# Four graph layers on one core: a third row buffer for the first two layers, and three small moves around it

## The chip, the core and the metric

The kernel runs on one core of a Trainium2 chip. A core has five engines that run their own instruction queues in order: TensorE (PE; its weight loads are shown as PEld), VectorE (DVE), ScalarE (ACT), GpSimd (POOL) and SyncE (SP), which here only issues DMA transfers. They meet at semaphores. The metric is device time in microseconds, the median of several runs.

## The reference, cut to what matters

Sixteen graphs of 1024 nodes with 128 features go through four layers. Each layer first normalises every node's features and clips at zero, and adds its result to `x`.

```python
h = relu(layernorm(x));  x = x + L0(h, adj, adj)   # rows: sum_i adj[i,j] h[i] / sum(adj[j,:]), two weights, relu
h = relu(layernorm(x));  x = x + L1(h, adj)        # (adj / row sums) @ h @ W1, leaky relu
h = relu(layernorm(x));  x = x + L2(h, adj)        # two rounds of an edge network: sigmoid scores on
                                                   # the edges, messages, a two-layer update, a layernorm
h = relu(layernorm(x));  x = x + L3(h, adj)        # attention: exp over the edges, row sums, elu
```

L2 needs, for each pair of nodes with an edge, `relu(a[i] + b[j]) . w` and its sigmoid. The graph has few edges, so the kernel compresses each 128x128 block of the adjacency to at most 320 slots (480 on the diagonal) by matrices of zeros and ones that TensorE multiplies with.

## The kernel before, in words

One graph is a *batch*. Its work is cut into three pieces, each a generator that emits instructions and yields a weight of progress:

- `first` (L721): layers 0 and 1, the norm ahead of layer 2, and then `build` (L828), which makes the 0/1 matrices `on`, `onT`, `om`, `omT` of 36 blocks (28 off the diagonal, 8 on it), four blocks to a group, nine groups.
- `main` (L1169): layer 2. Each of its two rounds (`round`, L890) walks over the nine groups: `gather` (L991, matmuls `pre` at L1001, ACT and DVE make `hid` at L1017 and L1018), `dots` (L1034), `scores` (L1060, DVE's `val` at L1091), `scatter` (L1096, matmuls `p` at L1113, DVE's `upd` at L1121) and `messages` (L1130). Between the rounds `between` (L1152) updates the nodes by halves.
- `last` (L1199): the end of layer 2 and layer 3.

`run` (L1225) weaves three batches into one another: while `main` works on batch b, `last` ends batch b-1 and `first` starts batch b+1. The weave decides in which order instructions are emitted; the framework then gives out buffers and orders each engine's queue by that emission order, by what is ready and by which buffers it takes to be free. The order is fixed in the program. Buffers with one tag form a ring: `bufs` says how many, and a tile waits until an older one of its tag has had its last reader.

What the change touches:

- **Row buffers** (`N_ROW`, L36; `row`, L694; `load`, L688). A row buffer of 4 KB per partition holds one strip of the adjacency. Layer 0 reads for each of eight tiles t a row strip `at` and a column strip `ct` (loads at L738 and L742, recorded at L691); layer 1 reads a strip `l` of the transposed matrix. All of them come from the tag `rowa` with two buffers. For `at`, ACT sums the rows (L744, output `tn`, sum `deg`), TensorE transposes it (L748), ACT copies the halves out (L749), and the result is stored (L751, `adjT<-tn`). For `ct`, DVE takes the pattern of edges (L756, `has`) and TensorE multiplies it with the features (`neighbours`, L290, `nb`), and DVE adds the product, scaled by the reciprocal `rdeg` of the row sum, to `own` (L315).
- **The reciprocal** of the row sum stands at L745, between ACT's sum and the transposes.
- **Spare hot buffers** (`MORE_OFF`, L39; `hot_tile`, L798). The 0/1 matrices of the 28 blocks off the diagonal have 28 + 4 buffers of each of the four kinds, so that `build` for the next batch can run ahead of `main`, which still reads the old ones. Those on the diagonal have eight and no spare.
- **Norm statistics** (`spread`, L227): per-partition statistics from eight (or four) `bn_stats`, then seven small DVE instructions of 8 (or 4) elements, a power of -0.5 on POOL (L243) in their midst, and one more small instruction in `normal` (L250) before ACT may normalise (L252). `spread` runs eight times per batch: ahead of each of the four layers (`normal`), and in four half updates (`update`, L338).
- **The half update of half 1**. `between` starts by loading the features of its half from DRAM (`back`, L717, shown at L718 as `xm<-xT`). `main` makes the generator at L1195 but takes its first step only in the second round, at the first group.
- **Weights**: `we2_rows` (L106, L111) has its own buffer for the whole kernel though only `fold_weights` uses it.

Of the kernel before, what the change touches and what calls it, by code (L numbers as in the profile page):

```python
# [9 lines left out]
F32 = mybir.dt.float32  # L10
# [4 lines left out]
OP = mybir.AluOpType  # L15
AX = mybir.AxisListType

LN_EPS = 1e-5
# [14 lines left out]

LANES = ("m", "a", "c")
N_SCRATCH = {"m": 5, "a": 4, "c": 5}
N_ROW = {"m": 2, "a": 2, "c": 1}  # L36
N_HID = 6

MORE_OFF = 4  # L39
MORE_DIAG = 0  # L40


# [9 lines left out]
def tile_four_gnn_layers(  # L52
# [22 lines left out]
    nc = tc.nc  # L75
    B, N, D = x.shape
    P = 128
# [3 lines left out]
    L = we1.shape[0]  # L81
# [10 lines left out]
    const = ctx.enter_context(tc.tile_pool(name="const", bufs=1))  # L92
# [10 lines left out]
    nc.scalar.dma_start(b0_bc, b0[None, :].broadcast_to([P, D]))  # L103
    we1_sb = const.tile([P, L, 2, D], F32, name="we1_sb")
    we2_sb = const.tile([P, L], F32, name="we2_sb")
    we2_rows = const.tile([P, L, D], F32, name="we2_rows")  # L106
    be1_sb = const.tile([P, L], F32, name="be1_sb")
    scale_sb = const.tile([P, L, 2], F32, name="scale_sb")
    with nc.allow_non_contiguous_dma(reason="small columns of weights, once"):
        nc.scalar.dma_start(we2_sb, we2.rearrange("l d o -> d (l o)"))  # L110
        nc.scalar.dma_start(we2_rows, we2.rearrange("l d o -> (o l) d")[None].broadcast_to([P, L, D]))  # L111
        nc.scalar.dma_start(be1_sb, be1.rearrange("l d -> d l"))
        nc.scalar.dma_start(scale_sb[:, :, 0], gamma.rearrange("l d -> d l"))
        nc.scalar.dma_start(scale_sb[:, :, 1], beta.rearrange("l d -> d l"))
# [41 lines left out]
            nc.tensor.transpose(wT_ps[:, k], w01_sb[:, k], ident)  # L156
        nc.vector.tensor_copy(wT, wT_ps)

    def fold_weights():


        signs = slide[:, :, G - 1]
        nc.scalar.activation(signs, we2_sb, AF.Sign)
        nc.vector.tensor_mul(we2_sb, we2_sb, signs)
        nc.vector.tensor_mul(be1_sb, be1_sb, we2_sb)
        nc.scalar.activation(we2_rows, we2_rows, AF.Abs)
        for l in range(L):
# [15 lines left out]
    def flat(t):  # L183
        return t.rearrange("p t d -> p (t d)")
# [4 lines left out]
    class Layers:  # L189
# [37 lines left out]
        def spread(self, src, name):  # L227

            n = src.shape[1]
            bn = self.small([P, T, 6], "bn", f"bn_{name}")[:, :n]  # L230
            for t in range(n):
                nc.vector.bn_stats(bn[:, t], src[:, t])

            st = self.small([P, 4, T], "stat", f"st_{name}")[:, :, :n]
            nc.vector.tensor_add(st[:, 0], bn[:, :, 1], bn[:, :, 4])
            nc.vector.tensor_sub(st[:, 1], bn[:, :, 1], bn[:, :, 4])
            nc.vector.tensor_add(st[:, 2], bn[:, :, 2], bn[:, :, 5])
            nc.vector.scalar_tensor_tensor(
                st[:, 1], st[:, 1], D / 4.0, st[:, 1], op0=OP.mult, op1=OP.mult
            )  # L240
            nc.vector.tensor_add(st[:, 1], st[:, 1], st[:, 2])
            nc.vector.tensor_scalar(st[:, 1], st[:, 1], 1.0 / D, LN_EPS, op0=OP.mult, op1=OP.add)
            nc.gpsimd.tensor_tensor(st[:, 2], st[:, 1], half_neg[:, :n], op=OP.pow)  # L243
            nc.vector.tensor_scalar(st[:, 0], st[:, 0], 0.5, None, op0=OP.mult)
            return st[:, 2], st[:, 0], st[:, 3]

        def normal(self, src, dst, func, name):

            rstd, mean, less = self.spread(src, name)
            nc.vector.scalar_tensor_tensor(less, mean, -1.0, rstd, op0=OP.mult, op1=OP.mult)  # L250
            for t in range(T):
                nc.scalar.activation(  # L252
                    dst[:, t], src[:, t], func, scale=rstd[:, t : t + 1], bias=less[:, t : t + 1]
                )
# [83 lines left out]
        def update(self, l, xf, xfT, msgT, dst, name):  # L338

            h2 = flat(self.scratch(f"h2s_{name}")).rearrange("p (k n) -> p k n", k=KB)  # L340
            for kb in range(KB):
                ps = self.one(f"h2_{name}_{kb}")
                for i, src in enumerate((xfT, msgT)):
                    nc.tensor.matmul(  # L344
                        ps, wu1_sb[:, l, i, kb * P : (kb + 1) * P], src,
                        start=(i == 0), stop=(i == 1),
                    )
                nc.scalar.activation(h2[:, kb], ps, AF.Relu, bias=bu1_sb[:, l, kb : kb + 1])
                yield 2
            new = self.scratch(f"xn_{name}")[:, :Q]  # L350
            ps = self.one(f"xn_{name}")
            for kb in range(KB):
                nc.tensor.matmul(
                    ps, wu2_sb[:, l, kb], h2[:, kb], start=(kb == 0), stop=(kb == KB - 1)
                )
            nc.scalar.activation(flat(new), ps, AF.Identity, bias=bu2_sb[:, l : l + 1])
            yield 2
            ps = self.one(f"tx_{name}").rearrange("p (t d) -> p t d", d=P)
            for t in range(Q):
                nc.tensor.transpose(ps[:, t], new[:, t], ident)  # L360
            nc.vector.tensor_add(dst, ps, xf)
            yield 1
            rstd, mean, _ = self.spread(dst, f"y_{name}")
            for t in range(Q):
                nc.vector.tensor_scalar(
                    dst[:, t], dst[:, t], mean[:, t : t + 1], rstd[:, t : t + 1],
                    op0=OP.subtract, op1=OP.mult,
                )
            yield 2
            nc.vector.tensor_mul(dst, dst, over_t(rows["gamma"][:, l], Q))  # L370
            nc.vector.tensor_add(dst, dst, over_t(rows["beta"][:, l], Q))
            yield 1
# [157 lines left out]
    class Edges:  # L530
# [76 lines left out]
        def scaled(self):  # L607

            con = self.con
            fold_weights()  # L610
            self.scale_terms()

            w3T = self.a.scratch("w3T")[:, 0]
            ps = self.a.one("w3T")[:, :P]
            nc.tensor.transpose(ps, w3_sb, ident)
            nc.vector.tensor_copy(w3T, ps)
            ps = self.a.one("v3")[:, :2]
            nc.tensor.matmul(ps, w3T, a3_sb, start=True, stop=True)
            nc.vector.tensor_copy(v3, ps)
            spread_v3(0)  # L620
            self.slide = con.tile([P, L, 2 * G - 1], F16, name="slide16")
            nc.vector.tensor_copy(self.slide, slide)
# [71 lines left out]
        def row(self, lane, name):  # L694
# [2 lines left out]
            self.n_rows += 1  # L697
            return self.work.tile([P, T, P], F32, tag=f"row{v}", name=name, bufs=N_ROW[v])

        def alone(self, lane, others):  # L700

            v = lane.lane
            lane.banks = [self.own[w] for w in others or v]
            lane.homes = [(f"h{w}", N_SCRATCH[w]) for w in others or v]
            self.rows_of[v] = others or v

        def columns(self, mat, t):
            return mat[:, t * P : (t + 1) * P].rearrange("(k p) n -> p k n", p=P)
# [12 lines left out]
        def first(self, b):  # L721
# [15 lines left out]
            for t in range(T):  # L737
# [4 lines left out]
                ct = self.load("a", self.columns(adj[b], t), f"ct_{b}_{t}")  # L742
                turned = lane.scratch(f"tn_{b}_{t}")
                nc.scalar.activation(turned, at, AF.Copy, accum_out=deg[:, 0, t : t + 1])  # L744
                nc.vector.reciprocal(rdeg[:, t : t + 1], deg[:, 0, t : t + 1])  # L745
                for ks, ps in lane.halves(f"tn_{b}_{t}"):
                    for i, k in enumerate(ks):
                        nc.tensor.transpose(ps[:, i], at[:, k], ident)  # L748
# [6 lines left out]
                for i, lo, hi in parts:  # L755
                    nc.vector.tensor_tensor(  # L756
                        has[:, i : i + hi - lo], ct[:, lo:hi], turned[:, lo:hi],
                        op=OP.logical_or, saturate=False,
                    )
                lane.layer0_tile(t, ct, z, own, rdeg, name)  # L760
                yield 2
            lane.layer0_end(xt, own)
# [406 lines left out]
        def main(self, s, b):  # L1169
# [7 lines left out]
            for l in range(L):  # L1177
# [11 lines left out]
                def half(h):  # L1189
                    return self.between(  # L1190
                        l, h, self.msg[h], s.xf[h], s.xT[h], xf[h], copy[h], f"{name}_{h}"
                    )

                yield from self.round(s, l, name, before, lambda: half(0))
                before = half(1)  # L1195
                s.xf, s.xT = xf, copy
            s.msg = self.msg

        def last(self, s, b):  # L1199


            def strip(k, lo, hi):
                n = (hi - lo) * P
                at = flat(self.row("c", f"a3_{b}_{lo}_{k}"))[:, : 2 * n].rearrange("p (k n) -> p k n", k=2)
# [230 lines left out]
```

## Time and profile before

| | before |
|---|---|
| time, median of 3 (range) | 5477.2 us (5474.47 to 5483.25) |
| profiled execution | 5482.0 us, granted TensorE clock 0.981 |
| PE busy | 5008.5 us, 91% |
| DVE busy | 4302.6 us, 78% |
| ACT busy | 3055.7 us, 56% |
| POOL busy | 174.4 us, 3% |
| DMA queue of SP | 545.58 MB, 33.7% of 16 engines' span |
| at, ct and l loads | 128 each of 512 KB; median 4.2, 4.5 and 4.3 us from issue to landing |

From the third batch on one weave takes about 331 us. Of the one that begins at 1148 us, layer 0's tiles take the time to 1243 us, layer 1 the time to 1313 us, and the building of the 0/1 matrices the rest to 1479 us; `main` runs beside all three. "Busy" is the time in which at least one instruction of an engine was under way. The view of waits lists what ended each idle stretch of an engine; the chain follows, from the last instruction back, what each step waited for.

### The profile page before, as it was taken

Reading aid. Unit: us, or ns where it says so; the run is one execution under the profiler, and the core shown is the slowest. Engines: PE = TensorE matmul, PEld = TensorE weight load, DVE = VectorE, ACT = ScalarE, POOL = GpSimd, SP = SyncE. Lnnn points to the kernel's source line nnn. Section 1 sums busy time; section 2 is a strip of 40 time slices with the busy share of each in tenths; the row PEclk is TensorE's granted clock in tenths of the full one; section 3 lists DMA queues with packets and bytes.
Section 4 is the critical chain, followed back from the end, with each engine's and each line's share of the span. In section 5 each row is a group of like instructions: output and inputs, shape, how many; then the busy total and the mean of one; then the engine's idle time right before and its main releaser. Section 6 shows DMA issues by size and latency. Waiting matters only on the chain.

```text
span 5482.0 us, 113604 instructions
## 1 busy us (share of the span) xinstructions
PE 5008.5 (91%) x45109; PEld 3741.4 (68%) x45109; DVE 4302.6 (78%) x10759; ACT 3055.7 (56%) x6790; POOL 174.4 (3%) x137
## 2 busy tenths in 40 slices
PE   5989999999999999999999999999999999999996
PEld 4666767667676766767667676676766666677664
DVE  3776787877879778797877878778797887978876
ACT  4556564655646556465555646556465564655543
POOL 0000000000000000000000000000000000000000
PEclk8999999999999999999999999999999999999998
DMA  6242415243252422424234142432424324243121
GB/s 176 63 138 83 124 57 144 78 128 104 73 145 66 135 90 86 137 70 126 91 107 126 57 144 79 125 106 72 146 65 137 90 87 133 68 128 92 54 63 51
DMA packets 740141, 554.56 MB, mean 101 GB/s; under 512 B 32273, under 2 KB 686353, under 8 KB 739601
## 3 DMA queue, kind: packets, MB, share of 16 engines
q1 hardware_dynamic: 734496, 545.58, 33.7%
q8 instruction: 356, 5.83, 0.4%
q10 hardware_dynamic: 5104, 1.65, 0.1%
q14 instruction: 185, 1.51, 0.1%
HBM read 446.44 MB, written 100.66 MB: 100 GB/s over the span
## 4 chain that ended last, share of the span: by engine, by line
PE 49%; DVE 28%; ACT 9%; DMA 8%; issue 4%; POOL 3%; SPq 0%; POOLq 0%; ACTq 0%; DVEq 0%
PE pre L1001 13%; DVE val L1091 8%; PE p L1113 6%; DMA at<-in_adj_dram 5%; DVE hid L1018 4%; PE msg L1130 4%; PE sc L1034 3%; PE bb L298 3%; PE h L344 3%; PE nb L290 3%; ACT hid L1017 2%; PE hp L507 2%; DVE omT L862 2%; POOL st L243 2%; PE pq L858 2%
## 5 line engine op out<-in xcount | busy, mean ns | idle before, releaser
L1018 DVE SCALAR_TENSOR_TENSOR hid<-pre,hid 128x320 f16<-128x320 f32 (+1 forms) x2048 | 1009.2, 507 | 327.5 <-ACT hid L1017 315.9
L1017 ACT ACTIVATE hid<-pre 128x320 f16<-128x320 f32 (+1 forms) x2048 | 906.4, 454 | 547.4 <-PE pre L1001 514.7
L1001 PEld LDWEIGHTS <-part 128*128 128x128 f16 x8192 | 748.6, 98 | 459.3 <-issue 236.6
L1001 PE MATMUL pre<-on,part 128*128 128x320 fp8e4 (+1 forms) x4096 | 970.1, 311 | 70.6 <-DVE hid L1018 62.3
L1001 PE MATMUL pre<-om,part 128*128 128x320 fp8e4 (+1 forms) x4096 | 987.4, 311 | 0.0
L1091 DVE TENSOR_TENSOR val<-onT,u 128x384 f32<-128x384 fp8e4 (+1 forms) x1152 | 603.4, 582 | 3.1
L1130 PE MATMUL msg<-upd,xf 128*128 128x128 f32 (+3 forms) x3008 | 604.7, 321 | 0.0
L1113 PE MATMUL p<-val,omT 128*128 128x128 f16 x6528 | 532.7, 220 | 43.0 <-DVE val L1091 33.7
L1113 PEld LDWEIGHTS <-omT 128*128 128x128 fp8e4 x6528 | 434.5, 97 | 111.5 <-DVE val L1091 42.0
L870 ACT ACTIVATE om<-pm 128x320 fp8e4<-128x320 f32 (+1 forms) x576 | 269.9, 469 | 351.4 <-PE pm L822 347.8
L1091 DVE TENSOR_TENSOR val<-omT,u 128x384 f32<-128x384 fp8e4 x896 | 443.4, 553 | 0.0
L1130 PEld LDWEIGHTS msg<-upd,xf 128*128 128x128 f32 x3008 | 409.8, 192 | 16.0 <-DVE upd L1121 3.0
L1121 DVE SCALAR_TENSOR_TENSOR upd<-p,adj 128x512 f32<-128x512 f32 x512 | 349.8, 683 | 80.8 <-PE p L1113 78.5
L1113 PE MATMUL p<-val,onT 128*128 128x128 f16 x4480 | 378.4, 220 | 0.5 <-DVE upd L1121 0.4
L507 PE MATMUL hp<-wh,e 128*128 128x129 f32 x2048 | 336.0, 289 | 25.5 <-DVE e L503 25.5
L854 ACT ACTIVATE onT<-pn 128x384 fp8e4<-128x384 f32 (+1 forms) x576 | 295.3, 513 | 114.0 <-PE pn L822 95.8
L1113 PEld LDWEIGHTS <-onT 128*128 128x128 fp8e4 x4480 | 307.8, 97 | 51.7 <-issue 16.5
L1055 ACT ACTIVATE srow<-sc,be_s,down 128x128 f32<-128x128 f32 (+2 forms) x512 | 254.6, 536 | 118.2 <-PE sc L1034 117.6
L507 PEld LDWEIGHTS hp<-wh,e 128*128 128x128 f32 x2048 | 281.3, 196 | 55.4 <-DVE e L503 29.8
L1034 PE MATMUL sc<-hid,slide 128*32 128x320 f16 (+1 forms) x4096 | 275.2, 317 | 27.5 <-DVE hid L1018 24.9
L862 DVE TENSOR_TENSOR omT<-pq,odd_off 128x384 fp8e4<-128x384 f32 x448 | 248.7, 555 | 57.5 <-PE pq L858 54.7
L744 ACT ACTIVATE tn<-at 128x1024 f32<-128x1024 f32 x128 | 135.3, 1057 | 270.5 <-DMA at<-in_adj_dram 238.8
(220 smaller groups left out, 8270.1 us busy)
## 6 DMA issues: line engine op xcount, KB each, us to landing
at<-in_adj_dram SPq DMA_DIRECT2D x128, 512.0 KB, 4.2
ct<-in_adj_dram SPq DMA_DIRECT2D x128, 512.0 KB, 4.5
adjT<-tn SPq DMA_DIRECT2D x128, 512.0 KB, 5.1
l<-adjT SPq DMA_DIRECT2D x128, 512.0 KB, 4.3
adj<-adjT SPq DMA_DIRECT2D x256, 256.0 KB, 3.6
a<-adjT SPq DMA_DIRECT2D x128, 384.0 KB, 3.2
adj<-adjT SPq DMA_DIRECT2D x448, 64.0 KB, 2.1
adj<-adjT SPq DMA_DIRECT2D x192, 128.0 KB, 2.6
```

The costliest lines, as they stand in the source:

```text
L507: nc.tensor.matmul(sums[:, t], e[:, i, t * P : (t + 1) * P], wh[:, k + i, : D + 1], start=False, stop=True, skip_group_check=True,)
L854: nc.scalar.activation(onT, pn[:, : ck * P], AF.Copy, saturate=False)
L862: nc.vector.tensor_tensor(omT.rearrange("p (k m) -> p k m", m=P), pq[:, :ck], self.odd[t == u][:, :, None].to_broadcast([P, ck, P]), op=OP ...
L870: nc.scalar.activation(om, pm[:, :c], AF.Copy, saturate=False)
L1001: nc.tensor.matmul(pre[:, :c], path.parts[node // Q][:, k, node % Q, v], hot[:, :c], start=(hot is on and k == 0), stop=(hot is om and k = ...
L1017: nc.scalar.activation(hid[:, 0, :c], pre[:, :c], AF.Relu)
L1018: nc.vector.scalar_tensor_tensor(hid[:, 1, :c], pre[:, :c], 0.0, hid[:, 0, :c], op0=OP.max, op1=OP.subtract)
L1034: ins = nc.tensor.matmul(self.sc[g * G : (g + 1) * G, : self.c], self.path.slide[:, self.l, G - 1 - r : 2 * G - 1 - r], self.hid[self.done ...
L1091: nc.vector.tensor_tensor(pair[:, i % 2, :ck], right[:, :ck], v.to_broadcast([P, ck, P]), op=OP.mult)
L1113: nc.tensor.matmul(self.ps[d][:, i], left[:, k], halves[:, k, :, h], start=(k, h) == terms[0], stop=(k, h) == terms[-1],)
L1121: nc.vector.scalar_tensor_tensor(upd, self.ps[d], S_SCALE, self.adj[:, d * Q : (d + 1) * Q], op0=OP.add, op1=OP.mult,)
L1130: nc.tensor.matmul(self.msg[h][:, (lo - h * Q) * P : (hi - h * Q) * P], self.xf[mb // Q][:, mb % Q], up, start=False, stop=True, skip_grou ...
```

## The change

- `rowa` gets a third buffer. To make room, `MORE_OFF` goes from 4 to 2 (two buffers fewer of each of the four kinds), `we2_rows` moves into a scratch buffer and is loaded when it is used, and the strip buffer of layer 3 gets a tag of its own of 3 KB in place of a row buffer of 4 KB.
- The row sum's reciprocal moves behind the copies and `has`, next to its first reader.
- `spread` takes four small DVE instructions ahead of POOL's power (six before), and one beside it (one before); the factor one half on the mean moves into `normal`'s instruction, and costs one small instruction in `update`.
- `main` takes the first step of half 1's `between` at the end of the first round, so that the load of its features is issued there.
- When one lane runs alone, it takes row buffers in the order a, a, m, a, m (five in all, as before with a, m, c, a, m).

```diff
-N_ROW = {"m": 2, "a": 2, "c": 1}
+N_ROW = {"m": 2, "a": 3, "c": 1}
-MORE_OFF = 4
+MORE_OFF = 2
...
-    def fold_weights():
+    def fold_weights(we2_rows):
...
+        nc.scalar.dma_start(we2_rows, we2.rearrange("l d o -> (o l) d")[None].broadcast_to([P, L, D]))
         nc.scalar.activation(we2_rows, we2_rows, AF.Abs)
...
+            nc.vector.tensor_sub(st[:, 1], bn[:, :, 1], bn[:, :, 4])
+            nc.vector.scalar_tensor_tensor(
+                st[:, 2], bn[:, :, 2], D * LN_EPS, bn[:, :, 5], op0=OP.add, op1=OP.add
+            )
+            nc.vector.scalar_tensor_tensor(st[:, 1], st[:, 1], 0.25, st[:, 1], op0=OP.mult, op1=OP.mult)
+            nc.vector.scalar_tensor_tensor(
+                st[:, 1], st[:, 2], 1.0 / D, st[:, 1], op0=OP.mult, op1=OP.add
+            )
+            nc.gpsimd.tensor_tensor(st[:, 2], st[:, 1], half_neg[:, :n], op=OP.pow)
             nc.vector.tensor_add(st[:, 0], bn[:, :, 1], bn[:, :, 4])
-            nc.vector.tensor_sub(st[:, 1], bn[:, :, 1], bn[:, :, 4])
-            nc.vector.tensor_add(st[:, 2], bn[:, :, 2], bn[:, :, 5])
-            nc.vector.scalar_tensor_tensor(
-                st[:, 1], st[:, 1], D / 4.0, st[:, 1], op0=OP.mult, op1=OP.mult
-            )
-            nc.vector.tensor_add(st[:, 1], st[:, 1], st[:, 2])
-            nc.vector.tensor_scalar(st[:, 1], st[:, 1], 1.0 / D, LN_EPS, op0=OP.mult, op1=OP.add)
-            nc.gpsimd.tensor_tensor(st[:, 2], st[:, 1], half_neg[:, :n], op=OP.pow)
-            nc.vector.tensor_scalar(st[:, 0], st[:, 0], 0.5, None, op0=OP.mult)
...
-            nc.vector.scalar_tensor_tensor(less, mean, -1.0, rstd, op0=OP.mult, op1=OP.mult)
+            nc.vector.scalar_tensor_tensor(less, mean2, -0.5, rstd, op0=OP.mult, op1=OP.mult)
...
+            nc.vector.tensor_scalar(mean, mean, 0.5, None, op0=OP.mult)
...
+        def strip(self, name):
+            if self.rows_of.get("c"):
+                return flat(self.row("c", name))
+            return self.work.tile([P, 2 * 3 * P], F32, tag="strip", name=name, bufs=1)
...
-            self.rows_of[v] = others or v
+            self.rows_of[v] = "aamam" if others else v
...
-                nc.vector.reciprocal(rdeg[:, t : t + 1], deg[:, 0, t : t + 1])
...
+                nc.vector.reciprocal(rdeg[:, t : t + 1], deg[:, 0, t : t + 1])
                 lane.layer0_tile(t, ct, z, own, rdeg, name)
...
                 before = half(1)
+                yield next(before)
```

More of the change, by code (lines that the diff above doesn't have):

```diff
@@ L105, in tile_four_gnn_layers @@
     we2_sb = const.tile([P, L], F32, name="we2_sb")
-    we2_rows = const.tile([P, L, D], F32, name="we2_rows")
     be1_sb = const.tile([P, L], F32, name="be1_sb")
@@ L110, in tile_four_gnn_layers @@
         nc.scalar.dma_start(we2_sb, we2.rearrange("l d o -> d (l o)"))
-        nc.scalar.dma_start(we2_rows, we2.rearrange("l d o -> (o l) d")[None].broadcast_to([P, L, D]))
         nc.scalar.dma_start(be1_sb, be1.rearrange("l d -> d l"))
@@ L234, in spread @@
             st = self.small([P, 4, T], "stat", f"st_{name}")[:, :, :n]
-            nc.vector.tensor_add(st[:, 0], bn[:, :, 1], bn[:, :, 4])
-            nc.vector.tensor_sub(st[:, 1], bn[:, :, 1], bn[:, :, 4])
-            nc.vector.tensor_add(st[:, 2], bn[:, :, 2], bn[:, :, 5])
-            nc.vector.scalar_tensor_tensor(
-                st[:, 1], st[:, 1], D / 4.0, st[:, 1], op0=OP.mult, op1=OP.mult
-            )
-            nc.vector.tensor_add(st[:, 1], st[:, 1], st[:, 2])
-            nc.vector.tensor_scalar(st[:, 1], st[:, 1], 1.0 / D, LN_EPS, op0=OP.mult, op1=OP.add)
-            nc.gpsimd.tensor_tensor(st[:, 2], st[:, 1], half_neg[:, :n], op=OP.pow)
-            nc.vector.tensor_scalar(st[:, 0], st[:, 0], 0.5, None, op0=OP.mult)
+            nc.vector.tensor_sub(st[:, 1], bn[:, :, 1], bn[:, :, 4])
[7 more added lines that the diff above has]
+            nc.gpsimd.tensor_tensor(st[:, 2], st[:, 1], half_neg[:, :n], op=OP.pow)
+            nc.vector.tensor_add(st[:, 0], bn[:, :, 1], bn[:, :, 4])
             return st[:, 2], st[:, 0], st[:, 3]
         def normal(self, src, dst, func, name):
-            rstd, mean, less = self.spread(src, name)
-            nc.vector.scalar_tensor_tensor(less, mean, -1.0, rstd, op0=OP.mult, op1=OP.mult)
+            rstd, mean2, less = self.spread(src, name)
+            nc.vector.scalar_tensor_tensor(less, mean2, -0.5, rstd, op0=OP.mult, op1=OP.mult)
             for t in range(T):
@@ L609, in scaled @@
             con = self.con
-            fold_weights()
+            fold_weights(self.c.scratch("we2_rows")[:, :L])
             self.scale_terms()
@@ L1203, in strip @@
                 n = (hi - lo) * P
-                at = flat(self.row("c", f"a3_{b}_{lo}_{k}"))[:, : 2 * n].rearrange("p (k n) -> p k n", k=2)
+                at = self.strip(f"a3_{b}_{lo}_{k}")[:, : 2 * n].rearrange("p (k n) -> p k n", k=2)
                 nc.sync.dma_start(
```

## The prediction

> **What bounds the kernel now.** I read the page from its engine table to its chain, then the windows of one weave, then the waits of ACT and SP inside it, then the timeline around one of those waits.
>
> ```profile
> PE 5008.5 (91%) x45109; PEld 3741.4 (68%) x45109; DVE 4302.6 (78%) x10759; ACT 3055.7 (56%) x6790; POOL 174.4 (3%) x137
> ...
> PE 49%; DVE 28%; ACT 9%; DMA 8%; issue 4%; POOL 3%; SPq 0%; POOLq 0%; ACTq 0%; DVEq 0%
> PE pre L1001 13%; DVE val L1091 8%; PE p L1113 6%; DMA at<-in_adj_dram 5%; DVE hid L1018 4%; PE msg L1130 4%; PE sc L1034 3%; PE bb L298 3%; PE h L344 3%; PE nb L290 3%; ACT hid L1017 2%; PE hp L507 2%; DVE omT L862 2%; POOL st L243 2%; PE pq L858 2%
> ```
>
> No engine carries the chain alone: TensorE has half of it. One load, `at`, has 5% of it (about 270 us of 5482), though all DMA together is at a third of its engines. The windows show the three stages of the weave that begins at 1148 us (columns: PE, PEld, DVE, ACT, POOL busy, granted clock, DMA share):
>
> ```profile
> 1148.00:1243.00 95.00, 89.31 (x820) 68.16 (x819) 71.70 (x189) 49.78 (x114) 2.64 (x2) 1.00 0.52 151
> 1243.00:1313.00 70.00, 67.35 (x560) 52.77 (x557) 48.32 (x121) 28.36 (x56) 2.64 (x2) 1.00 0.42 124
> 1313.00:1479.00 166.00, 153.51 (x1445) 110.93 (x1444) 147.55 (x362) 111.98 (x255) 5.45 (x4) 0.98 0.23 69
> ```
>
> In the tile stage DVE has 23 us and ACT 45 us to spare; in the building stage DVE is 89% busy. The chain of waits within the tile stage gives `at` 17.5% of its 95 us, 16.6 us: more than any other line there. The waits of ACT over the whole kernel and of SP's queue say why:
>
> ```profile
> ACT tn L744 <- DMA at<-in_adj_dram: 238.8, 93, 5.7
> ...
> DVE deg L745 <- ACT tn L744: 79.1, 63, 3.3
> ...
> SPq L691 <- PE tn L748: 830.8, 123, 26.9
> ...
> SPq L691 <- PE nb L290: 414.0, 156, 13.0
> ```
>
> ACT stands before 93 of 128 row sums until the strip lands. SP could not issue it: with two buffers, the next `at` waits for the transposes of this one. One instance, from the timeline:
>
> ```profile
> 1204.85 0.60 PE L748 MATMUL tn<-ident,at 128*128 128x128 f32 x4
> ...
> 1205.52 0.34 SPq L691 DMA_DIRECT2D at<-in_adj_dram  x1
> ...
> 1208.36 0.37 SPq L691 DMA_DIRECT2D ct<-in_adj_dram  x1
> ...
> 1209.57 1.06 ACT L744 ACTIVATE tn<-at 128x1024 f32<-128x1024 f32 x1 [2.55 <-DMA at<-in_adj_dram]
> ```
>
> The load goes out 0.07 us after the last transpose and lands 4 us later; ACT idles 2.55 us of them, with the `hid` behind it in its queue.
>
> **What the Trainium skill says.** (1) "Perfetto Trace Analysis", Identifying the Most-Contended Engine: matmul busy time misjudges TensorE, since matmuls are pipelined. The trace agrees: `pre` lasts 311 ns, but eight of them take 1.09 us on the chain, 0.136 us each, so 89 busy of 95 us is not full. (2) The same page, Optimization Strategy: the same bubble again and again can mean too few buffers for the next tile; 93 of 128 strips show it. (3) "DMA: Bandwidth & Descriptors", Anatomy of one DMA: about 2 us fixed plus bytes over 436 GB/s, 3.2 us for 512 KB; the trace's median of 4.2 us is used. (4) "Perfetto Trace Analysis", Optimizing Scalar/DVE Operations: some 60 ns of DVE per small instruction, with a profiled latency of about twice that. The trace has 166 ns for a statistics instruction, with starts 80 ns apart; 80 is used.
>
> **The change part by part.**
>
> *Third row buffer.* In the changed program's SP queue, `at` of tile t+1 stands behind the store of t-1 and waits for the product `nb` of t-1, no longer for the transposes of t. In the instance above that is the moment at which `ct` of the next tile went out in the earlier round (1198.02 us), 7.5 us ahead of 1205.52 and over the 4.2 us that it needs. So the wait of ACT, and with it most of DVE's wait at the reciprocal, goes. What is left sets the gain. TensorE's own pace in the tile stage, from counts of the groups in that window and spacings on the chain: 199 `pre` x 0.135 = 26.9, 128 `nb` x 0.115 = 14.7, 222 `p` x 0.057 = 12.7, 64 transposes x 0.11 = 7.0, `msg` 7.0, `sc` 3.5, the other 51 some 10 (512-wide ones at 0.45, the rest at 0.11 to 0.23): 82 us of 95. Layer 1's stage, counted likewise, needs 66.5 of 70: 95%. If the tile stage comes to that, it takes 82/0.95 = 86 us: 9 us less per weave. Thirteen weaves have a tile stage of 95 to 99 us; two (85 and 77 us) get 5 us; the first runs alone with five buffers before and after. 13 x 9 + 2 x 5 = **127 us**. Loads of `l` and `ct` come earlier too, but PE waited for them only 9.3 and 10.4 us in all: within that figure.
>
> *Reciprocal.* It waited for ACT 79.1 us because ACT waited for `at`; behind `has` it waits for something DVE has just waited for. What was queued behind it was `val` and `hid`. Its gain is inside the 9 us. Cost: nothing, the same 128 instructions of 159 ns.
>
> *Statistics.* 64 spreads in `normal` lose two instructions each and 64 in `update` one: 192 x 0.08 = 15.4 us of DVE. The way from the first of them to POOL was 1.17 us (1318.21 to 1319.38); two links of about 0.2 us fall out. Where nothing else fills TensorE (`PE tp L260 <- ACT xf L252`, 55.9 us in all), that shows in full; elsewhere DVE has room outside of the building stage. Between 0 and 0.08 x 12 + 4 x 0.4 = 2.6 us per batch; I take 0.7: **11 us**.
>
> *Half 1's first step.* `xm<-xT` is on the chain once per weave with 3.69 us, issued at 1301.95 us behind four loads of `adj`; PE waits for it 14.0 us in all. Issued some ten places earlier in SP's queue, it is there in time. Between 14 and 15 x 3.7 = 55 us; other chains lie close, so 1.5 us per weave: **22 us**.
>
> *Two spare buffers fewer.* A block's matrices now wait for the block two places back in the old batch's last round, not four. In the changed order, `onT`, `om` and `omT` stand 6 to 9 places later in their queues, about half a group. Today's waits for such a release are small: `DVE on L813 <- PE pre L1001` 23.9 us, and `ACT onT` for `val` 13.6. Lower bound 0, upper bound two blocks' making at the end of each weave (36 blocks take some 150 us of the building stage, 4 us each), 8 us x 15 = 120. I take 1 us per weave: a loss of **15 us**. The work that hides the rest is the diagonal group, which comes last and has no spare in either version.
>
> *Weights.* `we2_rows` is loaded where it is used: ACT, and then DVE and the scales behind it, wait for a landing of 2 to 4 us once, less 0.49 us of issue at the start: a loss of **2 us**. The strip's tag and the lone lanes' order keep their numbers of buffers: nothing.
>
> Sum: -127 - 11 - 22 + 15 + 2 = -143: 5477 - 143 = **5334, say 5335 us**.
>
> **The rivals.**
> - *The wait changes its name.* ACT comes to `tn` early, but TensorE's backlog of `p` and `msg` or DVE's eight `val` (3.75 us in one piece on the chain) then end last. For it: DVE has 12.5% of the stage's chain in `val`. Against it: DVE is 75% busy there. With 3 us per weave left of the 9: 45 + 11 + 1 for the load: 5420 us.
> - *The building stage pays.* DVE is at 89% there, and a late buffer stops an engine with everything queued behind it. With the small gain above (57 us) and 5.5 us lost in 15 weaves (83): 5503 us, slower. Against it: today's waits for these buffers are under 3 us per weave.
> - *All comes off.* The tile stage falls to TensorE's 82 us (13 us x 13 + 8 x 2 = 185), the load gives 3 us and the statistics 1.3 per batch, the building loses nothing: 185 + 45 + 21 - 2 = 249: 5228 us.
>
> **How the numbers follow.** Forecast 0.6, first rival 0.2, second 0.1, third 0.1. About a fifth of the instructions on each engine stand elsewhere, which spreads each case by some tens of us. The range, 5265 to 5445, leaves out the second and third rivals. Faster by over 0.2%: all but the second rival and a part of the first, 0.87; the same 0.04; slower 0.09.
>
> **What would show it.** Right: `ACT tn <- DMA at` falls from 238.8 to under 40 us, `at` leaves the chain, DVE's wait at the reciprocal falls under 20, the tile stage from 95 to 84 to 90 us, and layer 1 and building stay within 3 us of 70 and 166. Wrong: the tile stage stays at 93 or more with `val`, `hid` or `p` in the place of `at` on its chain (first rival), or the building stage grows past 170 us with waits of `on`, `onT`, `om` or `omT` for `pre`, `val` or `p` (second). `PE h <- DMA xm` should fall from 14.0 us to under 4.

## The result, and the profile after

The changed kernel takes **5407.2 us** (median of 4 runs, 5398.25 to 5413.14) against 5476.9 us (median of 4) of the kernel before on the same chip: a ratio of **0.987, 95% interval 0.9852 to 0.9887**. It is some 70 us faster. The forecast was 5335 us: the time lies in the range, but the gain is half of the one forecast (143 us), and it ends nearer to the first rival (5420 us, "the wait changes its name") than to the forecast.

The page of the changed kernel: the engine table, then the two lines of the chain (its shares by engine, then by line):

```profile
PE 5012.4 (93%) x45109; PEld 3743.8 (69%) x45109; DVE 4288.8 (79%) x10567; ACT 3055.3 (56%) x6790; POOL 176.5 (3%) x137
...
PE 61%; DVE 20%; ACT 10%; DMA 4%; POOL 2%; issue 2%; SPq 0%; ACTq 0%; POOLq 0%; DVEq 0%
PE pre L1008 15%; PE p L1120 7%; DVE val L1098 6%; PE nb L289 6%; PE msg L1137 5%; PE h L343 4%; PE hp L507 3%; PE bb L297 3%; PE sc L1041 3%; DVE hid L1025 3%; DMA at<-in_adj_dram 3%; PE pq L865 2%; PE pn L829 2%; POOL st L242 2%; ACT hid L1024 2%
```

Line numbers have shifted by 7 or so: the row sum is L751 now, its transposes L754, `pre` L1008. TensorE does the same 45109 matmuls in the same busy time; the span is 70.6 us shorter, and its share of the chain has grown from 49% to 61%, taken from DVE (28 to 20) and from DMA (8 to 4). `at` has fallen from 5% to 3% of the chain. DVE has 192 instructions and 13.8 us less.

The waits of the whole kernel (columns: us in all, times, longest):

```profile
ACT hid L1024 <- PE pre L1008: 679.5, 590, 6.5
...
DVE deg L766 <- ACT tn L751: 90.2, 81, 2.9
...
ACT tn L751 <- DMA at<-in_adj_dram: 66.1, 48, 4.5
...
DVE on L820 <- PE pre L1008: 52.2, 31, 1.9
```

And the line of the kernel before that the prediction didn't show:

```profile
ACT hid L1017 <- PE pre L1001: 514.7, 526, 4.6
```

The wait for `at` fell by 173 us (238.8 to 66.1). ACT's wait for `pre`, ahead of the `hid` that it shares with DVE, grew by 165 us. ACT's busy time is the same (3055.7 and 3055.3 us), so most of the time that it no longer stands before the strip it now stands before TensorE's next product. DVE's wait at the reciprocal did not fall (79.1 to 90.2).

One weave of the changed kernel, by the three stages (columns: PE, PEld, DVE, ACT, POOL busy, granted clock, DMA share, GB/s):

```profile
1134.10:1223.90 89.80, 86.42 (x808) 67.07 (x801) 68.69 (x181) 48.51 (x112) 2.64 (x2) 1.00 0.55 161
1223.90:1292.90 69.00, 66.95 (x555) 52.58 (x554) 47.69 (x116) 28.53 (x56) 2.64 (x2) 1.00 0.41 125
1292.90:1462.20 169.30, 157.65 (x1466) 112.71 (x1464) 150.54 (x361) 113.27 (x258) 5.60 (x4) 0.97 0.22 68
```

The tile stage is 6 us shorter, layer 1 a little, and the building stage 3 us longer. The counts show why a stage isn't an edit: against the prediction's windows of the kernel before, 12 matmuls (820 to 808) and 8 DVE instructions have left the tile stage of this weave, and the building stage has 21 matmuls more (1445 to 1466). Matmuls that are under way at a window's edge count in it; counted by their starts, from the first row sum to the last `own`, the tile stage has 820 before and 800 after, the building stage 1444 and 1464, in each of the twelve weaves averaged below. Layer 1 has 554 in every kernel, so its lengths can be compared. Those of the other two stages can be compared only where the counts agree: 800 and 1464 also hold for the changed kernel with two rows (and two or four spare), with the old statistics or the old place of the reciprocal, and for the kernel before with two spare, without and with the rows. Means over the 4th to the 15th weave, from the row sums' start and the last `own` and layer 1 outputs of each weave; "idle" is the time in which TensorE ran no matmul, all three stages together:

| kernel (the edits are told below) | tile stage | layer 1 | building | one weave | idle of TensorE |
|---|---|---|---|---|---|
| before | 97.1 | 70.6 | 165.7 | 333.4 | 22.9 |
| after | 90.6 | 69.2 | 168.4 | 328.2 | 17.9 |
| after, two rows | 91.8 | 69.1 | 167.4 | 328.3 | 19.8 |
| after, two rows, four spare | 91.9 | 69.1 | 168.7 | 329.6 | 19.3 |
| after, no first step | 90.1 | 70.5 | 168.1 | 328.7 | 18.9 |
| before, first step | 90.9 | 69.1 | 169.8 | 329.9 | 20.5 |
| before, two spare | 92.3 | 70.3 | 168.1 | 330.7 | 21.5 |
| before, rows and two spare | 91.3 | 70.0 | 167.8 | 329.1 | 19.4 |

From before to after a weave loses 5.2 us, and TensorE 5.0 us of idle time: the gain is idle time of TensorE, no work. The split is not exact: for the same 45109 matmuls the kernels below show between 4977 and 5024 us of busy time; why, no run shows. Twelve such weaves are 62 of the 70.6 us; the first three bring 6, what comes after them 2. Each row comes from one profiled execution, and executions of one kernel differ by some 15 us (about 1 us per weave), so the last tenths mean nothing; the ratios below decide. One number of these executions does follow the row buffers: in the tile stage alone TensorE is idle for 3.7 to 5.3 us per weave in the seven kernels with three (3.9 in the changed one) and for 5.8 to 7.3 us in the seven with two (7.1 before).

### The profile page after: what moved, and what is told of

Its sections match the earlier page's. It is cut to its first block, busy times and chain, and to the rows that moved or that the text cites. A ratio compares the mean times of both kernels' runs of the same rounds, so it can differ in the third digit from the quotient of the medians.

```text
span 5411.4 us, 113484 instructions
## 1 busy us (share of the span) xinstructions
PE 5012.4 (93%) x45109; PEld 3743.8 (69%) x45109; DVE 4288.8 (79%) x10567; ACT 3055.3 (56%) x6790; POOL 176.5 (3%) x137
## 4 chain that ended last, share of the span: by engine, by line
PE 61%; DVE 20%; ACT 10%; DMA 4%; POOL 2%; issue 2%; SPq 0%; ACTq 0%; POOLq 0%; DVEq 0%
PE pre L1008 15%; PE p L1120 7%; DVE val L1098 6%; PE nb L289 6%; PE msg L1137 5%; PE h L343 4%; PE hp L507 3%; PE bb L297 3%; PE sc L1041 3%; DVE hid L1025 3%; DMA at<-in_adj_dram 3%; PE pq L865 2%; PE pn L829 2%; POOL st L242 2%; ACT hid L1024 2%
## 5 line engine op out<-in xcount | busy, mean ns | idle before, releaser
L1024 ACT ACTIVATE hid<-pre 128x320 f16<-128x320 f32 (+1 forms) x2048 | 922.2, 456 | 713.5 <-PE pre L1008 679.5
L1008 PEld LDWEIGHTS <-part 128*128 128x128 f16 x8192 | 752.7, 99 | 429.3 <-issue 211.4
L1008 PE MATMUL pre<-on,part 128*128 128x320 fp8e4 (+1 forms) x4096 | 966.6, 311 | 42.5 <-DVE hid L1025 32.3
L1008 PE MATMUL pre<-om,part 128*128 128x320 fp8e4 (+1 forms) x4096 | 979.0, 312 | 0.0
L1137 PE MATMUL msg<-upd,xf 128*128 128x128 f32 (+3 forms) x3008 | 591.8, 320 | 0.0
L1041 PE MATMUL sc<-hid,slide 128*32 128x320 f16 (+1 forms) x4096 | 272.4, 320 | 29.9 <-DVE hid L1025 28.5
L820 DVE TENSOR_SCALAR on<-far,wid 128x384 fp8e4<-128x384 f16 (+1 forms) x576 | 238.6, 427 | 60.0 <-PE pre L1008 52.2
L816 ACT ACTIVATE far<-iota_off,mid 128x384 f16<-128x384 f16 x448 | 275.6, 629 | 11.8 <-DVE on L820 11.3
```

Source lines behind the costliest of these rows:

```text
L816: nc.scalar.activation(far[:, : ck * P], self.iota[t == u][:, : ck * P], AF.Abs, bias=s.mid[:, i : i + 1])
L1008: nc.tensor.matmul(pre[:, :c], path.parts[node // Q][:, k, node % Q, v], hot[:, :c], start=(hot is on and k == 0), stop=(hot is om and k = ...
L1024: nc.scalar.activation(hid[:, 0, :c], pre[:, :c], AF.Relu)
L1041: ins = nc.tensor.matmul(self.sc[g * G : (g + 1) * G, : self.c], self.path.slide[:, self.l, G - 1 - r : 2 * G - 1 - r], self.hid[self.done ...
L1137: nc.tensor.matmul(self.msg[h][:, (lo - h * Q) * P : (hi - h * Q) * P], self.xf[mb // Q][:, mb % Q], up, start=False, stop=True, skip_grou ...
```

## The experiments

The theories were: the third buffer carries the gain and what is missing was lost to the spare buffers; or the third buffer brings little, because ACT's wait was beside TensorE's work, and the gain comes from the smaller edits. Each kernel was compared with the kernel before on its own chip.

### Parts taken out of the changed kernel

**Two row buffers.** Everything of the change but the third buffer.

```diff
-N_ROW = {"m": 2, "a": 3, "c": 1}
+N_ROW = {"m": 2, "a": 2, "c": 1}
```

> The changed kernel with two row buffers instead of three, all else as changed (two spare hot buffers too). If the third row buffer is what shortens the tile stage (theory A): tile stage back from 90.6 to about 97 us per weave, building stays near 168, time about 5407 + 15 x 6.5 = 5500 us, slower than the kernel before. If the small edits (statistics, reciprocal, early load) did it and the buffer is idle memory (theory B): tile stage stays near 91, time 5400 to 5420 us.

Measured: 5427.8 us, ratio 0.9909 (0.9894 to 0.9924). The third buffer is worth 0.39% here, about 20 us (some 9 to 34 us, from the two intervals taken together); the rest of the change gains 50 us without it. The waits of this kernel:

```profile
ACT hid L1024 <- PE pre L1008: 560.3, 572, 4.7
...
ACT tn L751 <- DMA at<-in_adj_dram: 253.5, 104, 5.8
...
DVE deg L766 <- ACT tn L751: 66.9, 62, 3.1
```

ACT waits for `at` even longer than in the kernel before, 253.5 us, and the kernel is 50 us faster than that all the same. One line of code then takes away 187 us of this wait, brings back 119 us of it before `hid`, and gains 20 us. The tile stage of this kernel:

```profile
1139.50:1230.30 90.80, 85.80 (x804) 67.45 (x801) 68.29 (x181) 48.78 (x113) 2.64 (x2) 1.00 0.55 158
```

TensorE is busy for 94.5% of it, with the third buffer for 96.2% (86.42 of 89.80): that is what the buffer does. In the mean of the twelve weaves the idle time of this stage falls from 5.9 to 3.9 us, 2.0 us per weave or some 26 us over thirteen, which fits the 20 us. Both kernels have 800 matmuls in this stage by their starts, and it takes 91.8 us with two rows and 90.6 with three; the stage was short already.

**Two row buffers and four spare hot ones.** As above, and

```diff
-MORE_OFF = 2
+MORE_OFF = 4
```

> The changed kernel with two row buffers and four spare hot buffers, as before the change: only the statistics, the reciprocal's place, the early load and the late load of weights are left. Theory A with the spare buffers as the cause of the longer building stage: tile stage 97, layer 1 near 69.5, building back from 168.4 to 165 or 166, time 5450 to 5462 us. If the building stage grew for another cause (a lower granted clock, theory C), building stays at 168 beside four spare buffers and the time is near the run with two: 5495 us.

Measured: 5442.6 us, 0.9935 (0.9922 to 0.9949). With two spare buffers *more* the kernel is 15 us slower than the one above, on the same chip (the intervals overlap by 0.0002). So two more spare buffers cost time here; having two fewer lost none. And its building stage, with the four spare buffers of the kernel before, takes 168.7 us, not 165.7: the longer building stage isn't their doing.

**No spare hot buffer.** The changed kernel with

```diff
-MORE_OFF = 2
+MORE_OFF = 0
```

> The changed kernel with no spare hot buffer off the diagonal: each block is rebuilt only when the same block of the batch before has been read for the last time. If fewer spares keep helping: 5390 to 5400 us. If there is a best number and two is near it, waits of on, onT and omT for releases show up in the building stage, which grows from 168 to 171 us or more: 5425 to 5460 us.

Measured: 5437.7 us, 0.993 (0.9917 to 0.9944), some 31 us slower than the change. Tile and building stage of one weave:

```profile
1144.90:1228.90 84.00, 78.67 (x732) 61.86 (x729) 64.35 (x171) 44.37 (x104) 2.64 (x2) 1.00 0.57 173
...
1298.00:1475.20 177.20, 165.38 (x1537) 117.82 (x1536) 154.75 (x371) 116.46 (x265) 5.60 (x4) 0.98 0.21 65
```

The shortest tile stage of all kernels and the longest building stage: 76 matmuls have left the first and 71 more stand in the second. Judged by its tile stage this would be the best kernel. It is a warning against reading an edit's worth from one stage, and it shows a loss from too few spare buffers, as the prediction feared it, below two. The waits for a release that were expected with it hardly show, though (`DVE on` for `pre` 59.3 us, with two spare ones 52.2), so how the 31 us are lost stays open.

**Spare buffers of unequal number**, none for `on` and `om`, five for `onT` and `omT`, with the reciprocal in its old place:

```diff
-MORE_OFF = 2
+MORE_OFF = {"on": 0, "om": 0, "onT": 5, "omT": 5}
```

> The changed kernel with the reciprocals in their old place, and the spare buffers given to those that are released last: none for on and om, which a gather frees, five each for onT and omT, which the scatter a group later frees. Against the run with the reciprocals moved alone: if the late releases limit the building, 5 to 20 us faster; if the building is set by its own chain of onT, pq, omT, pm, the same within 5 us; if the waits of on for a gather are what counts, 10 to 30 us slower.

Measured: 5407.8 us, 0.9877 (0.9862 to 0.9892): no different from the change. The stages move again (tile stage 93.9, building 164.6 us, their sum within 1 us of the change's). As a better version it brings nothing.

**No early first step.**

```diff
                 before = half(1)
-                yield next(before)
```

> The changed kernel without the early first step of half 1: its features are loaded in the next round again. If the early load is worth what layer 1's stage gained: that stage goes from 69.2 back to 70.6 us, PE waits for xm about 14 us again, time 5407 + 15 x 1.5 = 5430 us. If the load was hidden beside other chains: within 5 us of 5407.

Measured: 5414.7 us, 0.9885 (0.987 to 0.9901). On top of the rest the step is worth about 8 us; the intervals overlap. The wait that it is made for comes back:

```profile
PE h L343 <- DMA xm<-xT: 11.6, 15, 2.2
```

In the changed kernel this line is gone; only 0.2 us of waiting for a load of `xm` remain, ahead of one weight load.

**Old statistics** in the changed kernel (`spread`, `normal` and `update` as before; the core of the edit):

```diff
+            nc.vector.tensor_add(st[:, 1], st[:, 1], st[:, 2])
+            nc.vector.tensor_scalar(st[:, 1], st[:, 1], 1.0 / D, LN_EPS, op0=OP.mult, op1=OP.add)
...
+            nc.vector.tensor_scalar(st[:, 0], st[:, 0], 0.5, None, op0=OP.mult)
```

> The changed kernel with the old seven statistics instructions per spread. 192 small DVE instructions more at 0.08 us. If they count where DVE is the fullest (the building stage) and at the norms that TensorE waits for: 5407 + 11 = 5418 us, up to 5407 + 40. If DVE's spare time hides them: within 5 us of 5407.

Measured: 5407.4 us, 0.9871 (0.9856 to 0.9886): nothing lost.

**Reciprocal in its old place**, behind the row sum:

```diff
                 nc.scalar.activation(turned, at, AF.Copy, accum_out=deg[:, 0, t : t + 1])
+                nc.vector.reciprocal(rdeg[:, t : t + 1], deg[:, 0, t : t + 1])
...
-                nc.vector.reciprocal(rdeg[:, t : t + 1], deg[:, 0, t : t + 1])
                 lane.layer0_tile(t, ct, z, own, rdeg, name)
```

> The changed kernel with the reciprocals back in their old place. Alone on the kernel before the move cost 8 us. If that holds with three rows too: 5400 us. If it depends on the order around it: within 5 us of 5407, since the reciprocal stands at the same distance ahead of its reader in seven tiles of eight.

Measured: 5403.2 us, 0.9865 (0.9849 to 0.988): not to be told from the change.

### Single parts put into the kernel before

**Two spare hot buffers** in place of four, alone:

```diff
-MORE_OFF = 4
+MORE_OFF = 2
```

> The kernel before with two spare hot buffers instead of four, nothing else: it splits the 58 us of the run with the rows alone into the third row buffer and the spare buffers. If the prediction's sign holds (fewer spares cost 15 us): 5495 us, and the third buffer alone is worth some 75 us. If fewer spares help, as the two runs with two rows say (4 to 2 gave 15 us): 5465 us, and the third buffer alone is worth some 45 us.

Measured: 5458.2 us, 0.9968 (0.9956 to 0.998): 18 us *faster*. Waits of this kernel:

```profile
ACT hid L1017 <- PE pre L1001: 561.0, 511, 4.6
...
ACT tn L744 <- DMA at<-in_adj_dram: 239.0, 100, 4.9
...
DVE on L813 <- PE pre L1001: 29.9, 30, 1.7
```

ACT's wait for `at` hasn't moved by a microsecond, and still the tile stage is 92.3 us instead of 97.1. DVE's wait for a hot buffer's release grew from 23.9 to 29.9 us only, and ACT's 13.6 us for `onT` are gone. Its tile stage has 800 matmuls (by their starts), as in the changed kernel, where the kernel before has 820.

**Third row buffer, two spare ones and the moves of memory** that make room (`N_ROW`, `MORE_OFF`, `we2_rows`, `strip`, the lone lanes' order), old statistics, no first step:

```diff
-N_ROW = {"m": 2, "a": 2, "c": 1}
+N_ROW = {"m": 2, "a": 3, "c": 1}
-MORE_OFF = 4
+MORE_OFF = 2
...
+            self.rows_of[v] = "aamam" if others else v
```

> The kernel before with the third row buffer and what makes room for it (two spare hot buffers, late load of the weights' rows, the smaller strip), but with the old statistics, the reciprocal in its old place and no early first step. Theory A of the prediction (ACT's wait for at is what counts): 5477 - 60 or more, under 5420 us. If ACT's wait costs little because other work lies beside it (the run with two rows lost only 20 us): 5445 to 5465 us, though ACT's wait for at falls from 239 to under 80 us.

Measured: 5421.7 us, 0.9895 (0.9881 to 0.9909): 58 us faster than before. Set against the kernel with two spare ones alone (0.9968), the third buffer and the moves of memory bring 0.73%, about 40 us (30 to 50): more than on top of the other edits, where the third buffer alone was put in or left out. The moves of memory were not run by themselves, so a part of the 40 us may be theirs. Waits and tile stage:

```profile
ACT hid L1023 <- PE pre L1007: 705.7, 535, 6.6
...
DVE deg L751 <- ACT tn L750: 93.0, 79, 11.1
ACT tn L750 <- DMA at<-in_adj_dram: 69.3, 48, 4.7
```

```profile
1139.50:1230.20 90.70, 86.61 (x808) 67.07 (x801) 69.57 (x186) 48.61 (x112) 2.88 (x2) 1.00 0.53 159
```

The wait for `at` falls as in the change, and the wait for `pre` is 191 us above that of the kernel before. Of these, 46 us came with the two spare buffers alone (561.0 above), where the wait for `at` did not move; 145 us came with the row buffer and the moves of memory. The exchange of the one wait for the other is thus mostly the row buffer's.

**First step** of half 1, alone:

```diff
                 before = half(1)
+                yield next(before)
```

> The kernel before with the early first step of half 1, nothing else. If the load is what it saves wherever it stands: as the changed kernel loses without it, 7 us, so 5470 us. If the early step also shifts where the half update falls in the weave (theory W), more than that: 5440 to 5460 us, with the tile stage shorter than 97 us.

Measured: 5435.7 us, 0.9924 (0.9911 to 0.9937): 42 us faster, with neither buffers nor statistics touched. Its wait for `at` is that of the kernel before, and its tile stage is as short as the changed kernel's:

```profile
ACT tn L744 <- DMA at<-in_adj_dram: 244.9, 98, 5.4
```

```profile
1140.70:1231.20 90.50, 83.84 (x800) 66.39 (x795) 68.72 (x184) 47.17 (x110) 2.64 (x2) 1.00 0.56 160
1231.20:1299.90 68.70, 66.68 (x555) 52.38 (x554) 47.90 (x119) 28.49 (x56) 2.64 (x2) 1.00 0.42 125
1299.90:1469.50 169.60, 158.49 (x1472) 113.40 (x1470) 151.12 (x368) 114.33 (x259) 5.45 (x4) 0.98 0.22 68
```

Set beside the kernel before, 20 matmuls have left this tile stage and 27 more stand in the building stage; TensorE's idle time in the tile stage is 7.0 us in the mean of the weaves, before 7.1. A part of what moved can be named: four of the `h` products of the updates ran in the tile stage of each of the twelve weaves before, none now. The idle time that it took away lies elsewhere: 1.1 us per weave in layer 1 and 1.2 in building. That is 2.4 of the 3.5 us by which the weave is shorter; why the step alone gives 42 us, three times TensorE's old wait for `xm`, is not shown beyond this.

**New statistics** alone (`spread`, `normal` and `update` of the changed kernel; the core):

```diff
-            nc.vector.tensor_add(st[:, 1], st[:, 1], st[:, 2])
-            nc.vector.tensor_scalar(st[:, 1], st[:, 1], 1.0 / D, LN_EPS, op0=OP.mult, op1=OP.add)
...
-            nc.vector.tensor_scalar(st[:, 0], st[:, 0], 0.5, None, op0=OP.mult)
```

> The kernel before with the four-pass statistics, nothing else. Undone in the changed kernel they were worth nothing. Theory S: within 8 us of 5477. If they only count while TensorE waits at the norms: TensorE's waits for the norm (xf and h, 100 us in all before) fall by 10 to 25 us, and so does the time.

Measured: 5470.8 us, 0.9982 (0.9976 to 0.9988): 10 us faster.

**Late reciprocal** alone:

```diff
-                nc.vector.reciprocal(rdeg[:, t : t + 1], deg[:, 0, t : t + 1])
...
+                nc.vector.reciprocal(rdeg[:, t : t + 1], deg[:, 0, t : t + 1])
                 lane.layer0_tile(t, ct, z, own, rdeg, name)
```

> The kernel before with the reciprocals moved behind the edge pattern, nothing else. The run with two rows and four spare buffers left 37 us of the gain to the small edits, and neither the statistics (0 us when undone) nor the early load (7 us) accounts for it. Theory R: DVE no longer stops at the reciprocal with edge-network work behind it: about 5477 - 25 = 5452 us. Theory S (the gain is of several edits together, each small): within 8 us of 5477.

Measured: 5485.5 us, 1.0015 (1.0007 to 1.0024): 8 us *slower*. The wait at it is still there:

```profile
DVE deg L759 <- ACT tn L744: 71.7, 62, 2.5
```

### What the twelve say together

| part | alone, on before | last, on top of the rest |
|---|---|---|
| third row buffer (with the moves of memory, where alone) | -40 us, given two spare ones | -20 us |
| four to two spare hot buffers | -18 us | -15 us (with two rows) |
| half 1's first step | -42 us | -8 us, not resolved |
| new statistics | -10 us | 0 |
| late reciprocal | +8 us | +3 us, not resolved |

Alone, the ratios add up to 1.84% (1.05 + 0.76 + 0.18 - 0.15); together they bring 1.30%: they overlap. That they buy in part the same idle time of TensorE is the likely reason, but no run isolates it. Three row buffers with one, three or four spare hot ones, and four row buffers, were not run.

## Why the prediction was right in its direction and wrong in its sizes

- **That the wait of ACT is a matter of buffers: right.** In the kernels with the third buffer the wait is 60 to 72 us, in those without it 239 to 259. The timeline of the changed kernel shows how (time, duration, instruction):

```profile
1157.07 0.83 PE L289 MATMUL nb<-z,ct 128*128 128x128 f32 x6
1157.93 0.35 SPq L691 DMA_DIRECT2D at<-in_adj_dram  x1
...
1161.57 1.06 ACT L751 ACTIVATE tn<-at 128x1024 f32<-128x1024 f32 x1
...
1162.75 0.16 DVE L766 RECIPROCAL deg<-deg 128x1 f32<-128x1 f32 x1
...
1170.40 0.49 PE L754 MATMUL tn<-ident,at 128*128 128x128 f32 x3
```

  The load goes out 0.03 us after a product `nb` ends, as forecast, and ACT's row sum shows no wait. But from the issue to the row sum it is still 3.64 us; over the twelve weaves the median is 4.5 us, before 4.4. What changed is that the row sum now stands well ahead of its transposes (9.2 us in their mean, before 4.6): the order was rebuilt around the new buffer, and the lead of the load was spent on an earlier row sum. So the load has no more room ahead of the row sum than before, and 48 strips are still waited for: 66.1 us, where under 40 were forecast, and 3% of the chain, which `at` was to leave.

- **127 us for the third buffer: the step that failed.** "If the tile stage comes to that, it takes 82/0.95 = 86 us" rests on TensorE's own pace, 82 us of 95. That pace came from the fastest stretches. The chain of the kernel before has three stretches of eight `pre` in this window:

```profile
1150.30 1.35 PE pre L1001 x8
...
1160.29 1.26 PE pre L1001 x8
...
1239.17 1.09 PE pre L1001 x8
```

  The prediction took the last. Over all its pieces in the window the chain has 83 `pre` in 13.06 us, 0.157 us each where 0.135 was used. With the chain's mean spacing for each of the groups that the prediction names, its own count gives some 91 us (an estimate), not 82. TensorE's busy time, 89.31 of 95.00 us, said the same: the idle rest was 5.7 us here and 7.1 us in the mean of the weaves, and the forecast took 9 us per weave out of it. The measured gain of the third buffer is 20 us last and at most 40 us alone, and what it took from the idle time of the stage is 2.0 us per weave (from two rows to three in the changed kernel). The Trainium skill ("Perfetto Trace Analysis", Identifying the Most-Contended Engine) says that matmul busy time doesn't measure how near TensorE is to its limit; that there was room for 13 us was the prediction's own step. In this stage no kernel came near it: a matmul of the changed kernel's tile stage takes 86.42/808 = 0.107 us of busy time, before 89.31/820 = 0.109, the lowest of all kernels is 83.84/800 = 0.105, and 82 us would have needed 0.100. Whether TensorE could go faster there was not tested.

- **173 us less of waiting for `at` are not 173 us less of time.** The rival "the wait changes its name" was right in kind: ACT's wait for `pre` grew by 165 us. With 3 us per weave for the buffer it gave 45 us, and the runs gave 20 to 40. The names were others than it said: `val` and `p`, which it expected last, went, in the weave shown, from 12.5% and 6.3% of the tile stage's chain to 11.9% and 5.4%, while `pre` went from 13.8% to 17.1% and `at` from 17.5% to 10.6%. The prediction gave this rival a chance of 0.2. The Trainium skill ("Perfetto Trace Analysis", Optimization Strategy) speaks of the same gap again and again "on the engine that should be saturated"; the prediction applied it to ACT, which is 56% busy. The gap was of buffers, as the page has it, but on an engine that wasn't the limit it was worth 20 us for 187 (two rows against three in the changed kernel).

- **The tile stage at 84 to 90 us: met in the mean (90.6), for another reason.** It was to show the third buffer's effect. But the first step alone gives 90.9, two spare buffers alone 92.3, and the change without its third buffer 91.8. The diagnostic didn't separate the theories, since work moves across the stage's border.

- **15 us lost by the spare buffers: wrong sign.** Two fewer gain 15 to 18 us. The loss that was priced comes only below two spare ones: with none it is 31 us. That two do better than four is measured. Why is not settled. On the kernel before, four of them put 20 more matmuls into the tile stage (820 and 800); but with two rows in the changed kernel the counts are the same with two spare as with four (800 and 1464), and the 15 us are lost all the same. So that spread is not what it needs.

- **Half 1's first step, 22 us: between the two measures**, 42 us alone and 8 last. The wait for `xm` went as forecast (14.0 to nothing on TensorE's matmuls), and layer 1's stage, with the same 554 matmuls, shrank by 1.5 us, just the 1.5 us per weave of the sum. What the prediction did not see is that the step moves work between the other two stages when it stands alone: the four `h` products leave the tile stage. On top of the rest it doesn't: two of them run there with the step and without it.

- **Statistics, 11 us: right alone (10 us), nothing on top of the rest.** DVE's busy time fell by 13.8 us where 15.4 was worked out.

- **Reciprocal at no cost: wrong.** The step "behind `has` it waits for something DVE has just waited for" read the program's text as the queue. In the timeline above the reciprocal runs at 1162.75, right behind the row sum and 7.6 us ahead of the strip's transposes, whose copies `has` needs: the framework put it where it was ready. So it kept its wait (90.2 us; in the kernel before with the late reciprocal, 71.7), and alone it costs 8 us; what makes the move slower, no run shows.

- **The building stage within 3 us of its old time: just met** (+2.7 us in the mean). Every kernel whose tile stage is under 93 us has such a longer building stage. Over thirteen weaves it is 35 us, where the sum had 15. The counts show 20 matmuls that moved in from the tile stage. The granted clock fell there too, 0.984 to 0.978, but isn't needed for it: without the first step the stage has 168.1 us at 0.986. The wait that was to show the second rival, `DVE on` for `pre`, grew from 23.9 to 52.2 us only.

- **Weights, 2 us lost:** the first row sum starts at 31.1 us, before at 31.4; no loss to be seen.

So of the 72 us between forecast and result the third buffer alone lost 87 to 107 (127 forecast, 20 to 40 measured), and the spare buffers, which gained 15 to 18 where a loss of 15 stood in the sum, gave some 30 back. That second error helped the first: with the measured 20 to 40 us for the third buffer and the rest of the sum as it stood, the forecast would have been 5421 to 5441 us, near the edge of the range (5445). That the measured time lies further inside is in part luck. What remains of the difference is the overlap of the parts, and not resolved.

## What to carry to other kernels

Before pricing a wait, look at the engine that carries the chain: ACT was busy for 56% of the span, and taking 187 us of waiting from it was worth 20 us, because it then waited for TensorE; the idle time that TensorE itself had in the stage (7.1 us of 97) was 92 us over thirteen weaves, less than the 127 us that were forecast. Price a pace from the mean of its stretches, not from the fastest. In a kernel whose stages overlap other work, compare counts of instructions per stage before crediting a shorter stage to an edit, and trust the sum. Fewer buffers that let one lane run ahead can gain, and their best number has to be measured (here two was better than none with three row buffers, and better than four with two).

## What the runs showed of the hardware

One thing was not expected. The four runs of the changed kernel had a mean granted clock of TensorE of 0.978, 0.978, 0.979 and 0.981, and spans of 5411.4, 5406.8, 5403.9 and 5396.5 us: 0.3% of clock goes with 0.27% of time, though TensorE has only 61% of the chain. Between kernels it doesn't hold so: the changed kernel with the old statistics had a mean of 0.981 at the same time (5407.4 us), and without the first step 0.983 at 5414.7 us. No run here sets the clock, so which follows which stays open.
